# A two-layer graph network: another order of products in the first pair, and TensorE in place of GpSimd and DMA in the last pair

## The chip, the cores and the metric

The kernel runs on one core of one Trainium2 chip. A core has TensorE (PE, matrix products), VectorE (DVE), ScalarE (ACT) and GpSimd (POOL), and SyncE (SP), whose queue issues the DMAs here. The metric is the device time of one execution in microseconds. [...]

## What is computed

64 graphs of 256 nodes with 512 features pass through two layers, each with a residual and a normalization over features. All is in 32-bit floats.

```python
def layer0(x, adj):                        # 8 heads of 64
    q, k, v = x @ Wq + bq, x @ Wk + bk, x @ Wv + bv
    scores = einsum('bqhd,bkhd->bhqk', q, k) / sqrt(64)
    attn = softmax(scores + (1 - adj) * -1e9)
    return einsum('bhqk,bkhd->bqhd', attn, v) @ Wo + bo

def layer1(x, adj):
    h = x @ W
    e = leaky_relu((h @ a1)[:, :, None] + (h @ a2)[:, None, :], 0.2)
    att = softmax(e * adj)
    return elu(att @ h + beta * h)

x = layernorm(x + layer0(x, adj))
x = layernorm(x + layer1(x, adj))
```

## The kernel before

**Tiling and stages.** The 64 graphs ("batches") are taken as 32 pairs. A pair is loaded and projected to queries, keys and values together (stages `x`, `q`, `k`, `v`), and then each of its two batches goes through `scores`, `sums` (the denominators of the softmax), `mix` (attention times values), `o` (projection with Wo, added to the residual X and normalized), `logits`, `attention`, `spread` (attention times X) and `u` (times W), after which `finish` applies the elu, adds, normalizes and stores. The digit behind a stage's name is the batch within the pair. The last pair holds batches 62 and 63.

**Seven products for eight.** `project` (its matmuls are at L433) computes a product of two matrices cut in quarters with seven block products, from sums and differences of the quarters. `left` and `right` are lists of seven operands. Products 1, 2 and 3 need untouched quarters on the right; 5 needs the first sum in place, 6 the second, 4 the last, and 7 the very first difference. GpSimd makes the sums of tokens in `token_sums` (L404) in the order t3, t1 (in place), t2, t4. The sums of Wq and Wk are made by VectorE in `streamed` (L366) in the first pair, and kept in memory for the later pairs. Products gather in PSUM accumulators: `ps_chain` takes 1, 6 and 7, `ps_cross` takes 5 and 3, and, where the first pair's queries and keys are made, `ps_second` takes 2 and `ps_fourth` takes 4. Parameter `raw` is true there.

**The plan.** Nothing is issued as it is written. Every operation is entered with `plan.op(engine, ns, function, reads, writes, mode, claims)`, and `Plan.place` settles the order in which all of them are emitted, by a model with durations and lags. For TensorE, each operation has a turn, (pair + `LATER[stage]`, index in `ROUND`), and all but the last `OPEN` = 60 TensorE operations are placed strictly by turn. The last 60 are placed by what can start soonest and, among those, by the longest remaining chain. The other engines' operations are placed when they are ready in the model, by due times that come from TensorE's turns. Buffers come from counted slots by tag (`half` 18, `full` 4, `ps` 8), and an operation can be placed only if all slots that it claims are free. An operation on TensorE with 0 ns and no instruction (as at stages `logits` and `attention`) only claims slots at its turn.

**Sums over keys.** After the scores, VectorE adds the mask (L750), ScalarE takes the exponential (L752), giving `pT` for each head with two blocks of 128 keys, and GpSimd adds the two blocks of each head into `both` (L754). TensorE multiplies `both` with ones to get the denominators (L766), VectorE takes the reciprocal (L778).

**The last batch.** Where `last` holds (batch 63), several steps go by TensorE instead of by memory: the reciprocals are spread over features with a selecting matrix (`ps_inv`, L802); `plain` projects without sums (L492 to L497); the row of logits comes by a transpose (`tr_s`, L933); the attention is transposed by TensorE (`tr_a`, L976) and copied by ScalarE (L979); `ps_y` (L1001) is its spread. For all other batches, batch 62 among them, a row of logits is made by a 32 x 32 transpose on VectorE (L940), a DMA to memory (`line`) and one back to all partitions (`row`); and the attention goes to memory (`square`, L983), comes back in four DMAs (`att_b`, L986), and is transposed in blocks by VectorE (L990). Where `last` holds, the two halves of the nodes also go through the logits' softmax apart.

**Constants of the second layer.** `second_layer_constants` clears `diag_sb` on GpSimd (L530), writes beta on its diagonal on VectorE (L532), and derives `wa_sb` from W and a.

**At the end** a check of the range of the softmax's sums decides whether a general form runs over all pairs again; with these inputs it doesn't.

Of the kernel before, what the change touches and what calls it, by code (L numbers as in the profile page):

```python
# [12 lines left out]
ALU = mybir.AluOpType  # L13
# [3 lines left out]
P = 128  # L17
# [9 lines left out]
         "o0": 0, "o1": 1, "logits0": 0, "logits1": 1, "attention0": 1, "attention1": 1, "spread0": 1, "spread1": 2,  # L27
         "u0": 1, "u1": 2}
SAFE = 1e15

# [23 lines left out]
class Plan:  # L54
# [12 lines left out]
    LATER = 15000.0  # L67
    OPEN = 60

# [158 lines left out]
def gnn_two_layers(ctx: ExitStack, tc: tile.TileContext, x, adj, Wq, bq, Wk, bk, Wv, bv, Wo, bo, W, a, beta, out):  # L228
    nc = tc.nc
# [128 lines left out]
    def streamed(w, w_dram, name):  # L358
# [3 lines left out]
        s1, s2, s3, s4 = ((lambda n=n: S[n][A]) for n in (1, 2, 3, 4))  # L362
        for n, to, p, m, op, reads in ((3, s3, w11, w21, ALU.subtract, [w]), (1, s1, w21, w22, ALU.add, [w]),
                                       (2, s2, s1, w11, ALU.subtract, [w, S[1]]),
                                       (4, s4, w12, s2, ALU.subtract, [w, S[2]])):
            plan.op("DVE", 700, lambda to=to, p=p, m=m, op=op: nc.vector.tensor_tensor(to(), p(), m(), op), reads,  # L366
                    [S[n]])
# [45 lines left out]

    def project(left, right, by_feature, claims, copy, add, inner=2, width=P, raw=False):

# [33 lines left out]
        copy((0, 0), pe(1, chain, True))  # L449
        if raw:  # L450
            add((0, 0), pe(2, second, True))
            copy((1, 0), pe(4, fourth, True))
        copy((1, 1), pe(5, cross, True))
        if not raw:
            add((0, 0), pe(2, second, True))
        copy((0, 1), pe(6, chain, False))
        add((0, 1), pe(3, cross, False))
        if not raw:
            copy((1, 0), pe(4, fourth, True) if second[1] is None else pe(4, fourth, False, [second]))
        acc = pe(7, chain, False)  # L460
# [68 lines left out]
    def second_layer_constants():  # L529
        plan.op("POOL", 500, lambda: nc.gpsimd.memset(diag_sb[A], 0.0), [], [diag_sb])  # L530
        for t in range(NT):
# [25 lines left out]
    def norm(X, ts):  # L557
# [22 lines left out]
        for i, t in enumerate(ts):  # L580
            plan.op("ACT", 810, lambda i=i, t=t: nc.scalar.activation(  # L581
                X[:, t, :], X[:, t, :], AF.Identity, bias=nm[:, i:i + 1], scale=rs[:, i:i + 1]),
                [nm, rs], [(X, (t, 0)), (X, (t, 1))])

    def pair(m, at, general=False):

        def turn(what):

            plan.turn = ((m or 0) + LATER[what], ROUND.index(what))

# [46 lines left out]
        def qk(left, bias, dst):  # L637
            project(left, right, True, [dst], *gather(
                lambda q: (lambda: dst[:, 2 * q[0]:2 * q[0] + 2, q[1] * N:(q[1] + 1) * N], (dst, q)), bias, True),
                width=N, raw=m == 0)  # L640

# [26 lines left out]
    def batch(m, s, qT, kT, V, dram, general):  # L668

        b = None if m is None else 2 * m + s  # L670
        last = b == B - 1 and not general
        X = sb("x", [NT, D], f"x_{b}")

        def turn(what):
            plan.turn = ((m or 0) + LATER[f"{what}{s}"], ROUND.index(f"{what}{s}"))

# [50 lines left out]
        def attention_by_keys():  # L727
# [6 lines left out]
            def scores(c):  # L734
# [4 lines left out]
                def pe():  # L739
                    for k in range(NT):  # L740
# [5 lines left out]
                plan.op("PE", 870, pe, [(m, (c // 2, j)) for m in (qT, kT) for j in range(NT)], acc, mode="rows",  # L746
                        claims=pT[2 * c:2 * c + 2] + [both[c]])
                for i in range(2):
                    h = 2 * c + i
                    plan.op("DVE", 690, lambda h=h, i=i: nc.vector.tensor_add(pT[h][A], acc[i][A], maskT_sb[A]),  # L750
                            [acc[i], maskT_sb], [pT[h]])
                    plan.op("ACT", 620, lambda h=h: nc.scalar.activation(  # L752
                        pT[h][A], pT[h][A], AF.Exp, scale=1.0 / HD ** 0.5), [pT[h]], [pT[h]])
                    plan.op("POOL", 725, lambda h=h, i=i: nc.gpsimd.tensor_tensor(  # L754
                        both[c][:, i, :], pT[h][:, 0, :], pT[h][:, 1, :], ALU.add),
                        [pT[h]], [(both[c], i)])

            def denominators():
# [4 lines left out]
                def pe():  # L763
                    for i in range(2):
                        for c in range(C):
                            nc.tensor.matmul(acc[32 * c:32 * c + 32, :], ones[:, 16 - 16 * i:48 - 16 * i],  # L766
                                             both[c][:, i, :], start=i == 0, stop=i == 1)

                plan.op("PE", 1000, pe, both, [acc], mode="sums", claims=[inv])

# [156 lines left out]
        turn("logits")  # L927
        if last:
            row = ps([N], "tr_s")
# [18 lines left out]

        for ts in ((0, 1), (1, 2)) if last else ((0, 2),):
            ts, k = slice(*ts), ts[1] - ts[0]  # L950
# [19 lines left out]
        turn("attention")  # L970
        if last:
            tra = ps([NT, N], "tr_a")
# [87 lines left out]

    plan.turn = (B // 2 + 1, 0)
    fine, row, least = st(1, "fine"), ps([P], "row"), st(1, "least")
# [18 lines left out]
    with tc.If(again != 0):  # L1081
# [3 lines left out]
        with tc.For_i(0, B, 2) as i:  # L1085
            for tile_ in stay:
                tile_.parts = {}
            plan = Plan({**slots, "half": slots["half"] - 1})
            pair(None, bass.ds(i, 2), general=True)
            order = plan.place()  # L1090
            with tc.manual_schedule():
                plan.emit(order)
# [29 lines left out]
```

## Time and profile before

| | us |
|---|---|
| median of 3 runs | 2735.23 (2733.61 to 2735.62) |
| time of the profiled execution | 2734.59 |
| its span | 2732.8 |
| TensorE busy | 2698.5 |
| VectorE busy | 1960.9 |
| GpSimd busy | 1728.6 |
| ScalarE busy | 1549.5 |
| mean granted TensorE clock | 0.995 of full |

Times in the profile count from the start of the span. The execution's own time is 1.8 us longer than its span. A line of the timeline reads: start, length, engine, source line, operation, output<-inputs, shapes, count, and in brackets how long the engine was idle before it and what released it. Lengths of grouped matmuls overlap the next group a little, since the end of each is modelled; the distance from start to start is what a group holds the engine. A matmul in 32-bit floats counts as two records.

### The profile page before, as it was taken

What the parts mean: (1) busy time and instruction counts of PE and PEld (TensorE: products, weight loads), DVE (VectorE), ACT (ScalarE), POOL (GpSimd) and SP (SyncE); (2) the same over time, 40 slices, a digit from 0 to 9 for tenths busy, and PEclk for the clock granted to TensorE, in tenths of its full rate; (3) what the DMA queues carried; (4) which work ended last, traced back from release to release, by engine and by line L of the source; (5) the groups of instructions that cost most, each with busy time, mean ns of one, the idle gap of its engine ahead of it and who ended that gap; (6) DMA issues with size and microseconds to landing.
All of it is one profiled execution on the core that took longest, in us unless ns stands there. A gap on an engine that the chain in (4) does not pass through costs nothing. (4 is left out here: it accounts for less than half of the span.)

```text
span 2732.8 us, 47289 instructions
## 1 busy us (share of the span) xinstructions
PE 2698.5 (99%) x15897; PEld 2268.1 (83%) x15897; DVE 1960.9 (72%) x3676; ACT 1549.5 (57%) x3712; POOL 1728.6 (63%) x2261
## 2 busy tenths in 40 slices
PE   9999999999999999999999999999999999999996
PEld 7888888888888888888888888888888888888874
DVE  6777777777777777777777776777777777767674
ACT  3456556556556565565565565655655655656554
POOL 4756666665676666666656766666666566665663
PEclk9999999999999999999999999999999999999998
DMA  8434434344443444343443434443444434343211
GB/s 234 104 101 128 119 97 114 97 121 124 100 120 96 109 128 118 94 113 99 124 124 98 120 90 115 128 113 99 111 101 120 128 96 118 89 120 113 80 55 54
DMA packets 581596, 301.44 MB, mean 110 GB/s; under 512 B 407020, under 2 KB 512356, under 8 KB 581348
## 3 DMA queue, kind: packets, MB, share of 16 engines
q1 hardware_dynamic: 581220, 298.34, 41.7%
q8 instruction: 130, 2.13, 0.3%
q14 instruction: 118, 0.97, 0.1%
q0 software_dynamic: 128, 0.01, 0.0%
HBM read 245.50 MB, written 52.75 MB: 109 GB/s over the span
## 5 line engine op out<-in xcount | busy, mean ns | idle before, releaser
L754 POOL TENSOR_TENSOR both<-pT 128x256 f32<-128x256 f32 x512 | 361.3, 734 | 398.6 <-ACT pT L752 398.6
L750 DVE TENSOR_TENSOR pT<-ps_sc,maskT_sb 128x512 f32<-128x512 f32 x512 | 324.2, 680 | 84.7 <-PE ps_sc L743 84.7
L752 ACT ACTIVATE pT<-pT 128x512 f32<-128x512 f32 x512 | 304.0, 626 | 49.3 <-DVE pT L750 47.4
L917 DVE SCALAR_TENSOR_TENSOR junk<-x,wa_sb 128x512 f32<-128x512 f32 x256 | 207.8, 837 | 110.3 <-ACT x L581 109.2
L743 PE MATMUL ps_sc<-qT,kT 64*128 64x256 f32 x2048 | 238.4, 382 | 0.0
L720 PE MATMUL ps_pv<-pT,v 128*64 128x256 f32 x2048 | 235.1, 382 | 0.0
L743 PEld LDWEIGHTS ps_sc<-qT,kT 64*128 64x128 f32 x2048 | 192.8, 187 | 44.4 <-issue 24.6
L469 ACT COPY u<-ps_chain 128x256 f32<-128x256 f32 x126 | 47.0, 373 | 319.2 <-PE ps_chain L433 318.7
L581 ACT ACTIVATE x<-x,nmr,rs 128x512 f32<-128x512 f32 x256 | 197.6, 808 | 50.2 <-POOL nmr L577 50.0
L720 PEld LDWEIGHTS ps_pv<-pT,v 128*64 128x64 f32 x2048 | 141.3, 137 | 91.0 <-DVE kT L478 12.8
L1026 POOL TENSOR_TENSOR X_sums<-x 128x256 f32<-128x256 f32 x126 | 150.9, 1207 | 99.5 <-ACT x L581 99.5
L564 ACT ACTIVATE junk<-x,mean 128x512 f32<-128x512 f32 x256 | 182.2, 714 | 6.4 <-DVE mean L570 6.4
L564 ACT ACTIVATE junk<-x 128x512 f32<-128x512 f32 x256 | 159.4, 625 | 36.5 <-DVE x L894 33.7
L704 POOL TENSOR_TENSOR x<-x,res_sb 128x512 f32<-128x512 f32 x128 | 176.3, 1380 | 0.0
L575 POOL TENSOR_SCALAR rs<-sq 128x2 f32<-128x2 f32 x130 | 34.9, 269 | 194.3 <-ACT junk L564 189.0
L404 POOL TENSOR_TENSOR oS<-oT 128x256 f32<-128x256 f32 x126 | 92.1, 731 | 84.2 <-DVE mean L570 52.5
L816 DVE TENSOR_TENSOR oT<-oT,inv_all 128x512 f32<-128x512 f32 x126 | 134.7, 1107 | 0.0
L955 POOL TENSOR_TENSOR e<-e,adj_sb 128x512 f32<-128x512 f32 (+1 forms) x65 | 81.6, 1255 | 80.7 <-DVE e L952 76.8
L433 PE MATMUL ps_chain<-sw_sb,yS 128*128 128x256 f32 x504 | 129.3, 379 | 0.0
L433 PE MATMUL ps_chain<-so_sb,oS 128*128 128x256 f32 x504 | 129.3, 379 | 0.0
L778 DVE RECIPROCAL inv<-ps_den 128x256 f32<-128x256 f32 x64 | 112.5, 1757 | 17.1 <-PE ps_den L766 8.7
L404 POOL TENSOR_TENSOR yS<-yT 128x256 f32<-128x256 f32 x126 | 92.6, 735 | 48.5 <-DVE yT L478 32.2
(240 smaller groups left out, 7164.5 us busy)
## 6 DMA issues: line engine op xcount, KB each, us to landing
x<-in_x_dram SPq DMA_DIRECT2D x64, 512.0 KB
out_dram<-x SPq DMA_DIRECT2D x128, 256.0 KB
inv_all<-rows SPq DMA_DIRECT2D x126, 256.0 KB
xin<-in_x_dram SPq DMA_DIRECT2D x248, 128.0 KB
wq_sums<-wq_sums SPq DMA_DIRECT2D x124, 256.0 KB
wk_sums<-wk_sums SPq DMA_DIRECT2D x124, 256.0 KB
wq_sums<-in_L_gnn_Wq_dram SPq DMA_DIRECT2D x93, 256.0 KB
wk_sums<-in_L_gnn_Wk_dram SPq DMA_DIRECT2D x93, 256.0 KB
```

What stands on the lines that cost most here:

```text
L404: plan.op("POOL", 180 + 545 * width // P, lambda: nc.gpsimd.tensor_tensor(dst(), p(), m(), ALU.subtract), reads, writes)
L433: nc.tensor.matmul(dst[:, f, :], lhs, rhs, start=start and f == 0 and c == 0, stop=c == inner - 1, skip_group_check=True)
L564: plan.op("ACT", 700, lambda: nc.scalar.activation(junk[A], X[:, t, :], func, bias=mean[:, i:i + 1] if bias else 0.0, accum_out=to[:, i:i ...
L581: plan.op("ACT", 810, lambda i=i, t=t: nc.scalar.activation(X[:, t, :], X[:, t, :], AF.Identity, bias=nm[:, i:i + 1], scale=rs[:, i:i + 1] ...
L704: plan.op("POOL", 1270, lambda t=t: nc.gpsimd.tensor_tensor(X[:, t, :], X[:, t, :], res_sb[A], ALU.add), [res_sb], tokens(t))
L720: nc.tensor.matmul(acc[r * HD:(r + 1) * HD, i, :], V[:, 2 * k + s, h * HD:(h + 1) * HD], pT[h][:, k, :], start=k == 0, stop=k == NT - 1)
L743: nc.tensor.matmul(acc[j][:, k, :], kT[r:r + HD, c, key_blk(k)], own(qT, r, c), start=True, stop=True)
L750: plan.op("DVE", 690, lambda h=h, i=i: nc.vector.tensor_add(pT[h][A], acc[i][A], maskT_sb[A]), [acc[i], maskT_sb], [pT[h]])
L752: plan.op("ACT", 620, lambda h=h: nc.scalar.activation(pT[h][A], pT[h][A], AF.Exp, scale=1.0 / HD ** 0.5), [pT[h]], [pT[h]])
L754: plan.op("POOL", 725, lambda h=h, i=i: nc.gpsimd.tensor_tensor(both[c][:, i, :], pT[h][:, 0, :], pT[h][:, 1, :], ALU.add), [pT[h]], [(bot ...
L917: plan.op("DVE", 780, lambda t=t, i=i, junk=junk: nc.vector.scalar_tensor_tensor(junk[A], X[:, t, :], 1.0, wa_sb[:, i, :], op0=ALU.mult, o ...
L1026: plan.op("POOL", ns, lambda: nc.gpsimd.tensor_tensor(dst(), p(), m(), op), reads, writes)
```

## The change

There are four parts.

1. In the first pair, queries and keys take their products in the order 1, 2, 5, 6, 4, 3, 7; before it was 1, 2, 4, 5, 6, 3, 7. `raw` is now called `first`. VectorE makes the sums of Wq and Wk in the order s1, s2, s4, s3 (before: s3, s1, s2, s4). The clearing of `diag_sb` reads `w_sb`, so it waits for that weight's load.
2. For batch 63, TensorE sums over all keys itself: the denominators take both blocks of every `pT` (16 matmul calls for 8), and GpSimd's additions into `both` are not made.
3. What `last` meant for the logits and the attention now holds where `near` does, for both batches of the last pair: row of logits and transposed attention by TensorE, softmax by halves. The spread, projections and finish of batch 62 stay as they were.
4. A tuple `FINISH` writes out the order of the last stages as (stage, pairs before the last); these stages get turns from it by `take_turn`. `OPEN` is 70 instead of 60.

```diff
+FINISH = (("sums1", 1), ("mix1", 1), ("scores0", 0), ("v", 0), ("attention0", 1), ("spread1", 2), ("sums0", 0), ("u1",
+          2), ("mix0", 0), ("scores1", 0), ("o1", 1), ("logits1", 1), ("o0", 0), ("attention1", 1), ("u0", 1),
+          ("spread1", 1), ("logits0", 0), ("spread0", 1), ("sums1", 0), ("mix1", 0), ("attention0", 0), ("spread0",
+          0), ("o1", 0), ("attention1", 0), ("u1", 1), ("u0", 0), ("logits1", 0), ("spread1", 0), ("u1", 0))
...
-    OPEN = 60
+    OPEN = 70
...
-        for n, to, p, m, op, reads in ((3, s3, w11, w21, ALU.subtract, [w]), (1, s1, w21, w22, ALU.add, [w]),
-                                       (2, s2, s1, w11, ALU.subtract, [w, S[1]]),
-                                       (4, s4, w12, s2, ALU.subtract, [w, S[2]])):
+        for n, to, p, m, op, reads in ((1, s1, w21, w22, ALU.add, [w]), (2, s2, s1, w11, ALU.subtract, [w, S[1]]),
+                                       (4, s4, w12, s2, ALU.subtract, [w, S[2]]), (3, s3, w11, w21, ALU.subtract, [w])):
...
         copy((0, 0), pe(1, chain, True))
-        if raw:
+        if first:
             add((0, 0), pe(2, second, True))
-            copy((1, 0), pe(4, fourth, True))
         copy((1, 1), pe(5, cross, True))
-        if not raw:
+        if not first:
             add((0, 0), pe(2, second, True))
         copy((0, 1), pe(6, chain, False))
-        add((0, 1), pe(3, cross, False))
-        if not raw:
-            copy((1, 0), pe(4, fourth, True) if second[1] is None else pe(4, fourth, False, [second]))
+        if not first:
+            add((0, 1), pe(3, cross, False))
+        copy((1, 0), pe(4, fourth, True) if second[1] is None else pe(4, fourth, False, [second]))
+        if first:
+            add((0, 1), pe(3, cross, False))
         acc = pe(7, chain, False)
...
-        plan.op("POOL", 500, lambda: nc.gpsimd.memset(diag_sb[A], 0.0), [], [diag_sb])
+        plan.op("POOL", 500, lambda: nc.gpsimd.memset(diag_sb[A], 0.0), [w_sb], [diag_sb])
...
+    def take_turn(m, what):
+        at_end = (what, B // 2 - 1 - m) if m is not None else None
+        if at_end in FINISH:
+            plan.turn = (B // 2 + 1, FINISH.index(at_end))
+        else:
+            plan.turn = ((m or 0) + LATER[what], ROUND.index(what))
...
+        near = m == B // 2 - 1 and not general
...
-                        claims=pT[2 * c:2 * c + 2] + [both[c]])
+                        claims=pT[2 * c:2 * c + 2] + ([] if last else [both[c]]))
...
-                    plan.op("POOL", 725, lambda h=h, i=i: nc.gpsimd.tensor_tensor(
-                        both[c][:, i, :], pT[h][:, 0, :], pT[h][:, 1, :], ALU.add),
-                        [pT[h]], [(both[c], i)])
+                    if not last:
+                        plan.op("POOL", 725, lambda h=h, i=i: nc.gpsimd.tensor_tensor(
+                            both[c][:, i, :], pT[h][:, 0, :], pT[h][:, 1, :], ALU.add),
+                            [pT[h]], [(both[c], i)])
...
-                    for i in range(2):
-                        for c in range(C):
-                            nc.tensor.matmul(acc[32 * c:32 * c + 32, :], ones[:, 16 - 16 * i:48 - 16 * i],
-                                             both[c][:, i, :], start=i == 0, stop=i == 1)
-
-                plan.op("PE", 1000, pe, both, [acc], mode="sums", claims=[inv])
+                    for k in range(NT if last else 1):
+                        for i in range(2):
+                            for c in range(C):
+                                nc.tensor.matmul(
+                                    acc[32 * c:32 * c + 32, :], ones[:, 16 - 16 * i:48 - 16 * i],
+                                    pT[2 * c + i][:, k, :] if last else both[c][:, i, :],
+                                    start=i == 0 and k == 0, stop=i == 1 and (k == NT - 1 or not last))
+
+                if last:
+                    plan.op("PE", 1500, pe, pT, [acc], mode="sums", claims=[inv])
+                else:
+                    plan.op("PE", 1000, pe, both, [acc], mode="sums", claims=[inv])
...
         turn("logits")
-        if last:
+        if near:
             row = ps([N], "tr_s")
...
-        for ts in ((0, 1), (1, 2)) if last else ((0, 2),):
+        for ts in ((0, 1), (1, 2)) if near else ((0, 2),):
...
         turn("attention")
-        if last:
+        if near:
             tra = ps([NT, N], "tr_a")
```

More of the change, by code (lines that the diff above doesn't have):

```diff
@@ L412, in token_sums, with project @@
                 (q[0, 1], keys(0, 1)), (t2, [(S, 0)]), (t3, [(S, 1)])]
-    def project(left, right, by_feature, claims, copy, add, inner=2, width=P, raw=False):
+    def project(left, right, by_feature, claims, copy, add, inner=2, width=P, first=False):
         shape = [2, width] if by_feature else [width // P, F]
@@ L583, in norm @@
                 [nm, rs], [(X, (t, 0)), (X, (t, 1))])
+    def take_turn(m, what):
[4 more added lines that the diff above has]
+            plan.turn = ((m or 0) + LATER[what], ROUND.index(what))
     def pair(m, at, general=False):
         def turn(what):
-            plan.turn = ((m or 0) + LATER[what], ROUND.index(what))
+            take_turn(m, what)
         def dram(ap, s):
@@ L639, in qk @@
                 lambda q: (lambda: dst[:, 2 * q[0]:2 * q[0] + 2, q[1] * N:(q[1] + 1) * N], (dst, q)), bias, True),
-                width=N, raw=m == 0)
+                width=N, first=m == 0)
         if m == 0:
@@ L671, in batch @@
         last = b == B - 1 and not general
+        near = m == B // 2 - 1 and not general
         X = sb("x", [NT, D], f"x_{b}")
         def turn(what):
-            plan.turn = ((m or 0) + LATER[f"{what}{s}"], ROUND.index(f"{what}{s}"))
+            take_turn(m, f"{what}{s}")
         def tokens(t):
@@ L1058, in gnn_two_layers @@
         pair(m, slice(2 * m, 2 * m + 2))
-    plan.turn = (B // 2 + 1, 0)
+    plan.turn = (B // 2 + 2, 0)
     fine, row, least = st(1, "fine"), ps([P], "row"), st(1, "least")
@@ L1088, in gnn_two_layers @@
             plan = Plan({**slots, "half": slots["half"] - 1})
+            plan.OPEN = 60
             pair(None, bass.ds(i, 2), general=True)
```

## The prediction

> **What bounds the kernel.** First I read the page's table of engines and its chain, then TensorE's instructions in order of time at both ends, then its waits.
>
> ```profile
> span 2732.8 us, 47289 instructions
> ...
> PE 2698.5 (99%) x15897; PEld 2268.1 (83%) x15897; DVE 1960.9 (72%) x3676; ACT 1549.5 (57%) x3712; POOL 1728.6 (63%) x2261
> ...
> PE 1%; DVE 0%; ACT 0%; POOL 0%; issue 0%; POOLq 0%; DVEq 0%; ACTq 0%
> ```
>
> TensorE (PE) is idle for 34 us in 2733, and the chain that ended last covers only the last 2% of the span. From 100 to 300 and from 2500 to 2640 us the windows show it fully busy, and the page's slices between show no gap. So an order of work can pay only at the two ends, where the change lies. First the opening, as TensorE's timeline and the windows of 2 us (window, length, busy time and count of PE, PEld, DVE, ACT, POOL, then granted clock, DMA share, GB/s):
>
> ```profile
> 10.04 2.24 PE L433 MATMUL ps_second<-xT,wq_sb 128*128 128x256 f32 x8
> 14.33 3.66 PE L433 MATMUL ps_fourth<-xS,wq_sb 128*128 128x256 f32 x8 [2.04 <-POOL xS L404]
> 17.83 1.89 PE L433 MATMUL ps_cross<-xT,wq_sums_s 128*128 128x256 f32 x8
> ```
> ```profile
> 12.00:14.00 2.00, 0.29 (x2) 0.00 (x0) 1.97 (x2) 0.00 (x0) 1.92 (x2) 1.00 1.06 409
> 14.00:16.00 2.00, 1.67 (x4) 1.40 (x5) 1.97 (x3) 0.00 (x0) 0.97 (x2) 0.58 1.04 402
> 16.00:18.00 2.00, 2.00 (x6) 1.61 (x6) 2.00 (x3) 0.00 (x0) 1.92 (x2) 0.56 1.07 392
> ```
>
> Product 4 waits 2.04 us for GpSimd's fourth token sum and then runs at clock 0.58 to 0.56: it holds PE 3.50 us (14.33 to 17.83), where eight records at full clock take 1.73 (17.83 to 19.56). Then the end, from the same timeline:
>
> ```profile
> 2629.28 3.72 PE L743 MATMUL ps_sc<-qT,kT 64*128 64x256 f32 x32
> ...
> 2658.26 1.07 PE L766 MATMUL ps_den<-both,ones 128*32 128x256 f32 x16
> 2662.18 2.94 PE L802 MATMUL ps_inv<-inv,select 128*128 128x256 f32 x8 [2.85 <-DVE select L783]
> ...
> 2678.18 0.68 PE L433 MATMUL ps_chain<-attT,x 128*128 128x128 f32 x4 [2.49 <-DVE attT L990]
> ...
> 2695.54 6.21 PE L1001 MATMUL ps_y<-attT,x 128*128 128x256 f32 x16 [0.68 <-ACT attT L979]
> ...
> 2717.07 1.03 PE L433 MATMUL ps_chain<-sw_sb,yS 128*128 128x256 f32 x4
> ```
>
> Call T0 the end of the last scores, 2632.93 us. The last matmul ends at T0+85.2; the last batch but one (62) then finishes in 14.7 us, and the span ends at T0+99.9. Full-clock PE work in those 85.2 us, from the spacing of starts: five projections by features or logits at 6.05 (30.3), three spreads at 3.1 (9.3), mixing 3.6, denominators 1.0, ps_inv 8 x 0.216 = 1.7, four plain halves at 3.45 (13.8), ps_y 16 x 0.216 = 3.5, small transposes 1.4: **64.6 us**. So 20.6 us are idleness or a slow clock (ps_inv takes 2.94 for 1.7, ps_y 6.21 for 3.5).
>
> **Part 1, opening.** Order 1, 2, 5, 6, 4, 3, 7 for 1, 2, 4, 5, 6, 3, 7; VectorE makes s1, s2, s4, s3 for s3, s1, s2, s4; the diagonal's clearing waits for w_sb, which takes the two diagonal writes (DVE L532, 1.20 us, started at 10.29 after beta's DMA) from before them. The last stall for wq_sb ends at 10.72. s1 starts there and takes 1.75 beside GpSimd, as L366 at 11.41 does: 12.5. s2 (1.63): 14.15. s4 (0.69): 14.85; s3 by 16.5. GpSimd's sums end at 9.86, 11.22, 12.61 and 14.28 now. Product 2 ends at 12.1. So 5 runs 12.55 to 14.28, 6 to 16.0, 4 to 17.7, 3 to 19.5, 7 to 21.2, against 24.74 now: **-3.5 us**. wk's subtractions follow directly on VectorE (17.75 to 22.86 now, some 2 us earlier then), ahead of k's fifth product at about 25.1. Behind this the queues hold the same work; PE's small stalls at 62 and 87 us (0.54 and 0.28) stay.
>
> Here a rule is weighed against a row. The Trainium skill, "TensorE: Matmul & The Clock Gate", in "What's actually happening", has the clock halve after about 3.4 us of idleness. By that, the 2.04 us stall would cost only itself and the change give 1.6 (2.04 less the 0.45 that remains before product 5). The row shows 0.58 after 2.04 us, so I add 1.8. The trace decides; 1.5 is kept as the lower end, and no idleness at all (-4.1) as the upper.
>
> The clearing of the diagonal sits on GpSimd's in-order queue behind a DMA issued at 32.7 to 35.8. Behind it would stand the sums over keys of the first scores (7 at 40.09). From the GB/s of the slices, w_sb lands near 40. These sums end at 46.7 and are read at 53.30: 6.6 us of cover, 3.1 after the earlier start. Price nothing; if it lands 5 us later than I think, 2 us.
>
> **Part 2, added and removed at the end.** Batch 63's sums over keys: 16 more records at 1.07/16: +1.0 on PE; gone are eight GpSimd adds (8 x 0.734 = 5.9 us) and four of 18 "half" slots that `inv` competed for. Batch 62's row of logits: +0.35 (tr_s: 0.34 in the chain); its attention: four transposes, +0.8 (tr_a: 2 x 0.41). **PE +2.2 us: 66.8.** ScalarE gets a copy (0.59), VectorE loses two transposes (0.24 and 0.70) and gains the split by halves (three extra short instructions, about 0.8); both lie beside PE.
>
> Off the path go batch 62's two trips through memory. Its scalars: svT ends at 2666.34, z starts at 2677.96: 11.6 us, of which the row's DMA stands behind four att_b issues in SP's queue. Its attention: e ends at 2686.30, attT is made at 2699.70: 13.4. A second rule here: the Trainium skill, "DMA: Bandwidth & Descriptors", in "Anatomy of one DMA", gives about 2.0 us fixed to a DMA (its fit is for another issuing path); two trips of two would be some 8 us. The rows show 25.0, since they hold the queue, the other engine's turn and the second wait. In their place come 0.8 and 1.4 us (tr_s to z; e to attT at 2695.49 of batch 63). So batch 62 is some 22 us earlier and no longer last.
>
> **Part 3, the order.** Up to the last scores it holds the same stages, so T0 moves only with the opening. Sums of 62 now stand before u of 60 (6 us earlier). Between spread of 60 and its u there is then 1.0 us of sums where products read sums that GpSimd makes: two yT adds and two GpSimd sums are about 2.4 us, less 1.0 and the first product's 0.86: a stall of 0.5 on PE. Behind T0 one projection (o of 61) stays fixed and 70 rather than 60 operations are placed by the longest remaining chain. Batch 63's own chain, unhindered, from the rows: exponentials ready at T0+6.5, sums 2.0, mixing and ps_inv 5.4, product 0.9, plain 6.9, norm 5, dots 1.4, softmax 6.0, attT 1.5, ps_y 3.5, copies 0.9, plain 6.9: PE done at T0+47. Now its sums come at T0+25.3. Batch 61's chain keeps its DMA: attention at T0+42 to 45, then about 12.8 to the end of u and 14.7: T0+72. So neither chain but **PE's work** is the bound: 66.8 and what idleness remains. I take 5 us of idleness, since until T0+42 only some 40 us of work can be ready and stages of 63 still meet VectorE and ScalarE, each about 55 us busy behind T0. Then the finish: 14.7 if a projection ends it, 12.2 if 63's plain product does (7.7 from 2712.83 to 2720.51, and 4.5 from the last normalization to the span's end): 13.5. Sum 66.8 + 5 + 13.5 = 85.3 for 99.9: **-14.6**. Bounds: idleness 1 and 12.2 give 80.0 (-19.9); idleness 12 and 14.7 give 93.5 (-6.4).
>
> **Sum.** -3.5 - 14.6 + 0.5 = -17.6. The profiled execution's time is 2734.59, 1.8 above its span, and 0.64 below the median; from the median 2735.23 I get 2717.6, in round numbers **2718 us**.
>
> **Rivals.**
> A. The tail is held by slots: batch 63's mixing takes a "full" slot, and now starts at 2654.66 as u of 60 has ended. If the order doesn't release one sooner, sums stay near T0+25. For: mixing came before the sums, as a queue for slots would have it. Against: spread of 60 moves behind, and four halves are freed. Batch 63's end then stays near T0+93 (2720.51+4.5), less 3.3 for the spread that stood before its last product (4.2, copies hide 0.9): about 90 with some cold clock as now, -10, but 62's spread and u (9.2) take perhaps half of it back: -5, with the opening -8: 2727.
> B. It doesn't do what it says: the chain through 61's DMA takes the gain at the end, or 62 and 63 now meet on VectorE and ScalarE (both 70% busy in a tail of 80 us). Then opening alone: 2732.
> C. Slower: SP's queue is in order, and 61's row, square and four att_b stand in it among outputs that wait for their batch. If 61's attT comes late, all later is late: attT at 2678.03 now leads to 27.5 us more. It decides from attT at T0+75.7 (99.9 + 3.3 - 27.5), 31 us later than now; by 40 us, +9: 2744. For: issues of 61 stood 1.1 to 4 us in that queue. Against: nothing in the trace waits for SP by tens of us.
>
> **Chances.** Forecast 0.73, A 0.14, B 0.08, C 0.05. Range 2709 to 2729: from -24 (both best ends) with 2 us for what I can't see, to A with its own 2 us. A measurement of this kernel can't tell changes within 0.2% (5.5 us). Faster: forecast, and nearly all of A: 0.86; same: B and the rest: 0.09; slower: 0.05.
>
> **What would show it.** Opening: product 5 directly behind 2, no clock below 1.0 from 12 to 18, the first ps_sc near 34 rather than 37.36. Sums of 63 within 12 us of T0; no line or square DMA for 62; ps_inv and ps_y near 1.7 and 3.5 us; last matmul near T0+72. Wrong if PE is idle for 12 us or more behind T0, or if another wait of several us stands between 100 us and T0.

## The result and the profile after

| | before | after |
|---|---|---|
| median of 6 runs (lowest to highest), us | 2734.31 (2732.43 to 2735.62) | 2720.05 (2719.03 to 2722.51) |
| span of the profiled execution, us | 2732.8 | 2718.3 |
| first score product (ps_sc) starts | 37.36 | 33.99 |
| T0, the end of the last scores | 2632.93 | 2631.01 |
| denominators of batch 63 start | T0+25.3 | T0+14.3 |
| last matmul ends | T0+85.2 | T0+75.2 |
| from there to the end of the span | 14.7 | 12.1 |

The ratio of the medians is 0.995 with a 95% interval of 0.9937 to 0.9963: the changed kernel is faster by 14.3 us, and the spans differ by 14.5. T0 moved by 1.9 us, the part behind T0 shrank from 99.9 to 87.3, by 12.6.

The page of the changed kernel, its table of engines and its chain:

```profile
span 2718.3 us, 47307 instructions
...
PE 2696.2 (99%) x15919; PEld 2268.6 (83%) x15919; DVE 1956.4 (72%) x3677; ACT 1548.9 (57%) x3713; POOL 1721.8 (63%) x2254
...
PE 97%; DVE 1%; POOL 0%; ACT 0%; issue 0%; DMA 0%; SPq 0%; ACTq 0%; POOLq 0%; DVEq 0%
```

TensorE does slightly less busy time in a shorter span: 22 us are left in which it is idle, against 34. TensorE's timeline at the opening (start, length, engine, line, output from inputs, tile, count; an idle time ahead of a row would stand in brackets):

```profile
11.01 1.89 PE L437 MATMUL ps_second<-xT,wq_sb 128*128 128x256 f32 x8
12.74 1.89 PE L437 MATMUL ps_cross<-xT,wq_sums_s 128*128 128x256 f32 x8
14.46 1.89 PE L437 MATMUL ps_chain<-xS,wq_sums_s 128*128 128x256 f32 x8
16.19 1.89 PE L437 MATMUL ps_fourth<-xS,wq_sb 128*128 128x256 f32 x8
```

Products 2, 5, 6 and 4 start 1.72 to 1.73 us apart, with no bracket. The windows of 2 us from 8 to 20 show a granted clock of 1.00 in every one (for the time up to 10.36 see below, at e4). The same timeline behind T0:

```profile
2631.01 1.13 PE L437 MATMUL ps_chain<-wo_sb,oT 128*128 128x256 f32 x4
...
2645.36 1.93 PE L781 MATMUL ps_den<-pT,ones 128*32 128x256 f32 x32
2647.22 3.67 PE L733 MATMUL ps_pv<-pT,v 128*64 128x256 f32 x32
2650.82 1.99 PE L822 MATMUL ps_inv<-inv,select 128*128 128x256 f32 x8
...
2669.92 0.41 PE L996 MATMUL tr_a<-ident,e 128*128 128x128 f32 x2 [1.41 <-DVE rc L983]
2670.51 0.41 PE L996 MATMUL tr_a<-ident,e 128*128 128x128 f32 x2 [0.18 <-DVE e L986]
2672.39 0.91 PE L437 MATMUL ps_chain<-attT,x 128*128 128x128 f32 x4 [1.47 <-ACT attT L999]
...
2694.72 3.69 PE L1021 MATMUL ps_y<-attT,x 128*128 128x256 f32 x16
...
2704.28 1.88 PE L502 MATMUL ps_plain<-w_sb,yT 128*128 128x512 f32 x4
```

Batch 63's denominators come 11 us sooner, ps_inv and ps_y run without a wait and at full pace (before: 2.94 and 6.21 us), and the last product is 63's own plain one. One hole is left, from 2668.4 to 2672.4, and two waits of half a microsecond. The waits of 2.85, 1.94, 2.49, 1.53, 1.24 and 0.68 us, which stood behind T0 before, are gone. SyncE's queue of DMA issues shows what is left of the trips through memory:

```profile
2646.54 0.59 SPq L961 DMA_DIRECT2D line<-svT  x1
2648.33 0.33 SPq L963 DMA_DIRECT2D row<-line  x1
2665.89 0.37 SPq L1003 DMA_DIRECT2D square<-e  x1
2668.25 2.61 SPq L1006 DMA_DIRECT2D att_b<-square  x4
```

They are batch 61's alone; batch 62 has none.

### The profile page after: what moved, and what is told of

The parts are those of the page before. It is cut to its first block, busy times and chain, and to the rows that moved or that the text cites. A ratio compares the mean times of both kernels' runs of the same rounds, so it can differ in the third digit from the quotient of the medians.

```text
span 2718.3 us, 47307 instructions
## 1 busy us (share of the span) xinstructions
PE 2696.2 (99%) x15919; PEld 2268.6 (83%) x15919; DVE 1956.4 (72%) x3677; ACT 1548.9 (57%) x3713; POOL 1721.8 (63%) x2254
## 3 DMA queue, kind: packets, MB, share of 16 engines
q8 instruction: 130, 2.13, 0.3%
## 4 chain that ended last, share of the span: by engine, by line
PE 97%; DVE 1%; POOL 0%; ACT 0%; issue 0%; DMA 0%; SPq 0%; ACTq 0%; POOLq 0%; DVEq 0%
PE ps_chain L437 33%; PE ps_cross L437 22%; PE ps_pair L437 10%; PE ps_sc L756 8%; PE ps_pv L733 8%; PE ps_second L437 6%; PE ps_fourth L437 6%; PE ps_den L781 2%; DVE junk L543 0%; DMA xin<-in_x_dram 0%; ACT junk L569 0%; DMA row<-line 0%; SPq L631 0%; PE ps_y L1021 0%; PE ps_plain L502 0%
## 5 line engine op out<-in xcount | busy, mean ns | idle before, releaser
L768 POOL TENSOR_TENSOR both<-pT 128x256 f32<-128x256 f32 x504 | 354.6, 731 | 383.1 <-ACT pT L765 383.1
L580 POOL TENSOR_SCALAR rs<-sq 128x2 f32<-128x2 f32 (+1 forms) x130 | 34.8, 268 | 208.8 <-ACT junk L569 203.5
L975 POOL TENSOR_TENSOR e<-e,adj_sb 128x512 f32<-128x512 f32 (+1 forms) x66 | 82.2, 1247 | 77.0 <-DVE e L972 77.0
L798 DVE RECIPROCAL inv<-ps_den 128x256 f32<-128x256 f32 x64 | 112.5, 1758 | 18.5 <-ACT junk L794 9.3
```

## The experiments

All times are medians with their ratio to the kernel before, measured on the same chip beside it (its own median there was 2733.89 to 2734.43). "Full" is the changed kernel, 2720.05. The profiled execution of each kernel gives the middle columns.

| kernel | parts | median, us | ratio (95%) | 63's denominators | PE idle behind T0 | last matmul | finish |
|---|---|---|---|---|---|---|---|
| before | none | 2734.31 | 1 | T0+25.3 | 12.4 | T0+85.2 | 14.7 |
| e1_opening | 1 | 2731.49 | 0.9992 (0.9983 to 1.0001) | 25.3 | 12.4 | 85.2 | 14.8 |
| e3_sums | 2 | 2731.30 | 0.9990 (0.9983 to 0.9997) | 25.6 | 12.1 | 83.7 | 14.1 |
| e2_near | 3 | 2728.68 | 0.9980 (0.9972 to 0.9987) | 25.6 | 9.1 | 81.4 | 13.8 |
| e4_order | 4 | 2731.64 | 0.9989 (0.9980 to 0.9998) | 25.4 | 11.1 | 82.2 | 14.6 |
| e8_no_near | 1, 2, 4 | 2738.82 | 1.0017 (1.0010 to 1.0024) | 25.3 | 14.7 | 87.0 | 18.5 |
| e6_no_order | 1, 2, 3 | 2725.68 | 0.9969 (0.9957 to 0.9980) | 21.9 | 9.1 | 79.6 | 11.7 |
| e11_open70 | 1, 2, 3, OPEN | 2724.39 | 0.9961 (0.9946 to 0.9975) | 21.5 | 8.2 | 78.9 | 12.3 |
| e7_no_sums | 1, 3, 4 | 2724.28 | 0.9961 (0.9947 to 0.9975) | 25.4 | 8.1 | 79.6 | 12.2 |
| e15_sums_slots | e7, slots | 2720.55 | 0.9951 (0.9934 to 0.9967) | 16.9 | 5.9 | 75.7 | 12.2 |
| after | 1 to 4 | 2720.05 | 0.9950 (0.9937 to 0.9963) | 14.3 | 4.2 | 75.2 | 12.1 |
| e13_products | full, sums back | 2719.52 | 0.9947 (0.9931 to 0.9964) | 14.3 | 4.8 | 73.1 | 12.0 |
| e12_near61 | full, 61 too | 2720.34 | 0.9949 (0.9933 to 0.9966) | 14.3 | 4.5 | 73.7 | 13.8 |
| e16_search | e12, slots, order | 2715.00 | 0.9930 (0.9913 to 0.9946) | 10.4 | 1.7 | 64.0 | 11.6 |

### One part alone: e1, e2, e3, e4

Each puts one part of the change into the kernel before. e1:

```diff
-            copy((1, 0), pe(4, fourth, True))
...
+        copy((1, 0), pe(4, fourth, True) if second[1] is None else pe(4, fourth, False, [second]))
+        if first:
+            add((0, 1), pe(3, cross, False))
```

> Part 1 alone on the kernel before: another order of the first pair's products, VectorE's order of the weight sums, the later clearing of the diagonal. My theory (stall of product 4 and the slow clock behind it): first scores near 34.0 us of the span for 37.36, some of it lost again in small stalls on the way, last scores of the last pair end 2.5 to 3.4 us before 2632.93, and the span ends as much earlier: 2729.5 to 2730.5. Rival (the end is set by other things than TensorE's queue, such as the DMAs of the last stages): the opening gains 3.4, the end less than 1: about 2732.5.

e2:

```diff
+        near = m == B // 2 - 1 and not general
...
-        if last:
+        if near:
```

> Part 3 alone: batch 62's row of logits and its attention by TensorE, order and sums as before. My theory (batch 62's two trips through memory are what ends last): batch 62 is finished some 20 us earlier, batch 63's plain products end the kernel, span 2722 to 2727. Rival (slots and the model's order hold the tail, not the DMAs): gain below 3, about 2731.

e3:

```diff
+                if last:
+                    plan.op("PE", 1500, pe, pT, [acc], mode="sums", claims=[inv])
```

> Part 2 alone: batch 63's sums over keys by TensorE, no additions on GpSimd, the four slots of these sums free. My theory: batch 63's denominators come sooner, but batch 62 with its DMAs still ends last, so within 1.5 us of before, plus or minus: 2731.5 to 2734.5. Rival (the slots were what held the tail): denominators within 15 us of the last scores and 5 us or more gained: 2728 or less.

e4:

```diff
-    OPEN = 60
+    OPEN = 70
...
+            take_turn(m, what)
```

> Part 4 alone: the written order of the last stages and 70 rather than 60 operations placed freely; batch 62 still by DMA, sums by GpSimd. My theory: denominators of 62 come about 6 us earlier and with them all of batch 62, whose two trips through memory still end last: gain 4 to 7 us, span 2726 to 2729. Rival (the order brings most of the whole change's tail by itself): 11 us or more, 2722 or less. Second rival: the order was made for the other parts and without them costs: slower than 2733.

Measured: -2.6, -5.4, -2.8 and -2.4 us, a sum of 13.1 for 14.3. That the sum is near doesn't make the parts independent: in none of the four do 63's denominators come before T0+25.3, and in the full change they come at T0+14.3. What made them come is in no part alone.

Against what was expected: e2's span of 2726.9 lies just inside the range. e4 gained 2.4 us and not 4 to 7. e3 gained a little more than forecast, but its denominators did not come sooner, which was the reason given. e1's median fits its range, though its interval just reaches 1; its trace does not, since the profiled execution was its slowest (2733.66), with the first scores at 36.14 and T0 only 1.0 us sooner.

These kernels also say something on the clock in the opening. e2, e3 and e4 have the old opening, each in an execution of its own. TensorE's timeline of e4:

```profile
8.67 3.31 PE L437 MATMUL ps_chain<-xT,wq_sb 128*128 128x256 f32 x8
11.81 1.89 PE L437 MATMUL ps_second<-xT,wq_sb 128*128 128x256 f32 x8
15.61 1.99 PE L437 MATMUL ps_fourth<-xS,wq_sb 128*128 128x256 f32 x8 [1.91 <-POOL xS L408]
```

The wait for the fourth token sum is there, 1.91 us for 2.04, but product 4 then holds PE 1.83 us (15.61 to 17.44), not 3.50, at clock 1.00. In e2 and e3 the waits are 1.75 and 1.29, with the same clock behind them. What differs is when the clock is decided. In each trace its records change only on a grid of 3.413 us, which lies elsewhere in each execution. Here are two steps of that grid before, and two in e4 (window, length, busy time and count of PE, PEld, DVE, ACT, POOL, granted clock, DMA share, GB/s):

```profile
10.92:14.33 3.41, 1.37 (x6) 0.86 (x5) 3.38 (x4) 0.00 (x0) 3.20 (x3) 1.00 1.06 407
14.33:17.74 3.41, 3.41 (x8) 2.78 (x9) 3.38 (x4) 0.00 (x0) 2.35 (x2) 0.50 1.05 401
```
```profile
11.36:14.77 3.41, 2.34 (x11) 1.71 (x9) 3.34 (x3) 0.84 (x2) 3.25 (x3) 1.00 1.05 405
14.77:18.18 3.41, 2.57 (x12) 2.29 (x13) 3.41 (x3) 0.54 (x2) 3.14 (x3) 1.00 1.06 399
```

Before, the stall lies whole in one step: PE is idle for 2.04 of 3.41 us, and the next step runs at half the clock. In e4 a boundary cuts the stall into 1.07 and 0.84 us, and the clock stays. In all fourteen traces, steps at full clock with up to 1.83 us of idleness were followed by full clock and those with 1.99 us or more by half; of two between, 1.88 us was followed by half (e6) and 1.89 by full (e4).

In those three, product 1 is stretched instead (3.14 us in e4, 2.13 before). The changed kernel has such a product 1 too, as its row and the durations of its records show (in ns, shortest/median/longest); the third row is product 4 of the kernel before, at half the clock:

```profile
8.05 3.12 PE L437 MATMUL ps_chain<-xT,wq_sb 128*128 128x256 f32 x8
```
```profile
L437 PE MATMUL ps_chain<-xT,wq_sb x8: 379/619/797, 8.1 to 10.8; 128*128 128x256 f32 x8
```
```profile
L433 PE MATMUL ps_fourth<-xS,wq_sb x8: 514/634/794, 14.3 to 17.5; 128*128 128x256 f32 x8
```

The column of the granted clock reads 1.00 over product 1, but the trace has no record of the clock ahead of 10.36 us in the changed kernel, 11.36 in e4 and 7.50 before. By their durations the stretched records ran at half the clock until then. In e2 and e3, waits of 0.25 and 0.69 us for wq_sb come on top.

From the start of product 1 to the first scores it is 29.45 us before, 28.30 to 28.47 in e2, e3 and e4, 25.94 after, and 25.65 to 27.31 in the nine other kernels with the new order. The first scores start at 36.73 to 37.36 us with the old order (mean of four 37.0) and at 33.92 to 36.14 with the new one (mean of ten 34.8). So the new order is worth about 2.2 us by the traces and 2.6 by e1's medians, and 3.5 only against the one execution that I worked from.

### One part undone: e8, e6, e7

> Parts 1, 2 and 4; batch 62 still by memory. My theory (its two trips of 11.6 and 13.4 us are on the path that ends last): most of the tail's gain is lost, span 2725 to 2729. Rival (batch 62 is early enough in the new order to hide them): 2720 or less.

> Parts 1, 2 and 3 without the written order (ROUND and 60 free operations as before). My theory (the tail is one schedule; batch 62's DMAs had to go before the other parts can pay, and the order only lets batch 63 start sooner): opening -2 to -3, near -5.4 as measured alone, sums little: span 2722 to 2726, so 4 to 8 us behind the full change. Rival (the parts simply add, each as alone): 2734.05 - 2.6 - 5.4 - 2.7 = 2723.3, minus 1.6 = span 2721.7. Second rival (order unneeded): within 2 us of the full change's 2718.3.

> Parts 1, 3 and 4; batch 63's key sums stay with GpSimd and its four slots. My theory (with the new order batch 63's denominators come some 14 us behind the last scores, and GpSimd's additions can be done by then): within 3 us of the full change, span 2717 to 2721. Rival (the four half slots keep the denominators back as before, to 20 us and more behind the last scores): 5 us or more lost, 2723 and above.

The edits are the full change with `if last:` back for `if near:` (e8), without `FINISH` and with `OPEN = 60` (e6), and with `both` summed by GpSimd and read by TensorE for batch 63 too (e7).

**Without part 3 the other three make the kernel slower than before** (e8, +4.4 us), where I had expected most of the gain to be lost (a span of 2725 to 2729 us; it is 2736.4). TensorE's timeline, its windows, one row of VectorE's timeline and SyncE's queue in e8:

```profile
2683.42 1.20 PE L436 MATMUL ps_chain<-attT,x 128*128 128x128 f32 x4 [7.12 <-issue]
```
```profile
2672.00:2676.00 4.00, 4.00 (x14) 2.31 (x13) 2.96 (x7) 2.33 (x7) 0.19 (x1) 1.00 0.49 86
2676.00:2682.60 6.60, 0.31 (x1) 0.00 (x0) 5.60 (x13) 5.39 (x16) 3.72 (x8) 0.71 0.01 2
2683.00:2687.00 4.00, 2.99 (x10) 2.62 (x11) 2.48 (x7) 1.77 (x3) 2.89 (x6) 0.50 0.40 146
```
```profile
2682.62 0.70 DVE L1008 STREAM_TRANSPOSE attT<-att_b 128x512 f32<-128x512 f32 x1
```
```profile
2669.91 0.37 SPq L1001 DMA_DIRECT2D square<-e  x1
...
2672.04 2.63 SPq L1004 DMA_DIRECT2D att_b<-square  x4
...
2685.08 0.38 SPq L1001 DMA_DIRECT2D square<-e  x1
2687.38 2.59 SPq L1004 DMA_DIRECT2D att_b<-square  x4
```

TensorE stands for 7.1 us until attT of 61 is made, and goes on at half the clock. "issue" names no releaser, but the product reads attT. Memory isn't all of that wait: the DMA engines, busy for 0.49 of the time from 2672 to 2676, are idle from there on (0.01), and attT is made only at 2682.62, behind work for 62 and 63 on VectorE (busy for 5.60 of 6.60 us). Batch 62's trip follows from 2685.08, fifteen us behind 61's, and its attention is made at 2698.0: it ends last, with a finish of 18.5. The written order has put 61 and 62 where nothing else is left to run beside them. This is akin to my third rival, with a smaller delay (61's attention is used at T0+52.5, the rival decided from T0+75.7) but for both batches, one behind the other.

Without part 4 (e6) 5.6 us of the gain are lost, as expected (4 to 8). Without part 2 (e7) it is 4.2, where I had expected less than 3 and the rival with the slots 5 or more. In both the denominators are late again. TensorE's timeline of e7:

```profile
2657.18 1.07 PE L778 MATMUL ps_den<-both,ones 128*32 128x256 f32 x16
2661.54 3.55 PE L814 MATMUL ps_inv<-inv,select 128*128 128x256 f32 x8 [3.29 <-DVE select L795]
...
2669.20 1.19 PE L496 MATMUL ps_plain<-wo_sb,oT 128*128 128x256 f32 x2 [3.41 <-DVE oT L825]
```

ps_den starts at T0+25.4, where it was before, though the order names the same stages; u of 60 has been used up ahead of it, so nothing fills TensorE while VectorE makes the reciprocals (3.29 us) and the features (3.41), and ps_inv then takes 3.55 us.

### Which of part 2's two gifts counts: e15, and which of part 4's: e11

Part 2 takes 5.9 us of additions from GpSimd and frees four "half" slots. e15 is e7, GpSimd's additions and all, with `both` of the last batch in another set of slots:

```diff
-            both = [sb("half", [2, N], "both") for c in range(C)]
+            both = [sb("piece" if last else "half", [2, N], "both") for c in range(C)]
```

> Parts 1, 3 and 4, with GpSimd's sums over keys of batch 63 kept, but put in four slots of another tag that is idle at the end, so the four half slots are free as in the full change. If the slots hold the denominators back: they come 14 to 16 us behind the last scores, span 2718 to 2720. If GpSimd's additions themselves, or the planner's rule that a change of TensorE's mode waits until nothing else is ready, hold them: 20 us and more behind the last scores, span 2721.5 to 2724. After the runs before I expect the second.

Its timeline:

```profile
2647.24 1.07 PE L778 MATMUL ps_den<-both,ones 128*32 128x256 f32 x16
2651.84 1.99 PE L814 MATMUL ps_inv<-inv,select 128*128 128x256 f32 x8
```

The 16 calls of the old form, fed by GpSimd, start at T0+16.9 instead of T0+25.4, ps_inv needs no wait, and 3.7 of the 4.2 us are back. I had expected the other outcome. So it is the slots that held batch 63, not the additions. The sums by TensorE are worth what is left, 0.5 us, which these runs can't tell from nothing.

e11 has the parts 1 to 3, the old order and `OPEN = 70`:

> Parts 1, 2 and 3 and 70 free operations, but turns by ROUND as before, so spread of batch 60 and o of 62 keep their place and the sums of 62 stand behind u of 60. Theory (what counts is that batch 63's stages may go ahead of the two batches before): within 2 us of the full change, span 2717 to 2720.5. Rival (the written order with the sums of 62 six us earlier counts): 3 to 6 us behind it, 2721 to 2724.

It is 4.3 us behind the full change, as the rival had it and not my theory, and 1.3 below e6 (five runs against seven, with ranges that overlap). The looser bound does little when it is added first (the denominators come at T0+21.5); the written order on top of it does the rest.

### VectorE's order in the opening: e13

```diff
-        for n, to, p, m, op, reads in ((1, s1, w21, w22, ALU.add, [w]), (2, s2, s1, w11, ALU.subtract, [w, S[1]]),
-                                       (4, s4, w12, s2, ALU.subtract, [w, S[2]]), (3, s3, w11, w21, ALU.subtract, [w])):
+        for n, to, p, m, op, reads in ((3, s3, w11, w21, ALU.subtract, [w]), (1, s1, w21, w22, ALU.add, [w]),
+                                       (2, s2, s1, w11, ALU.subtract, [w, S[1]]),
+                                       (4, s4, w12, s2, ALU.subtract, [w, S[2]])):
...
-        plan.op("POOL", 500, lambda: nc.gpsimd.memset(diag_sb[A], 0.0), [w_sb], [diag_sb])
+        plan.op("POOL", 500, lambda: nc.gpsimd.memset(diag_sb[A], 0.0), [], [diag_sb])
```

> The full change, but VectorE makes the weights' sums in the order of before (s3, s1, s2, s4) and the diagonal is written ahead of them as before; only the order of the products is new. My theory: s1 is ready at about 14.9 us as before, product 5 waits for it from 12.1 to 12.7 on, some 2.2 to 2.8 us idle, and the clock then halves as behind the stall before (0.58 there): first scores at 37.0 to 37.5, span 3 us above the full change. Rival [...]: only the wait is lost, no granted clock below 1.0 behind it, first scores near 36.2.

My expectation fell. VectorE's timeline of e13, and TensorE's row of product 5:

```profile
10.31 0.88 DVE L538 TENSOR_SCALAR diag_sb<-ident,beta_sb 128x128 f32<-128x128 f32 x2 [10.31 <-DMA beta_sb<-in_L_gnn_beta_dram]
11.33 1.54 DVE L371 TENSOR_TENSOR wq_sums_s<-wq_sb 128x512 f32<-128x512 f32 x1
12.90 1.64 DVE L371 TENSOR_TENSOR wq_sums_s<-wq_sums_s,wq_sb 128x512 f32<-128x512 f32 x1
```
```profile
13.54 1.89 PE L438 MATMUL ps_cross<-xT,wq_sums_s 128*128 128x256 f32 x8
```

s1 (it reads wq_sb alone) is still made first and s2, which reads s1 as well, behind it: the plan places these operations by when they are due, and the order in which the code names them decides nothing. The kernel before shows the same in its own trace, since the second of these rows reads a sum that the first has made:

```profile
11.41 1.75 DVE L366 TENSOR_TENSOR wq_sums_s<-wq_sb 128x512 f32<-128x512 f32 x1
13.19 1.63 DVE L366 TENSOR_TENSOR wq_sums_s<-wq_sums_s,wq_sb 128x512 f32<-128x512 f32 x1
```

So its sums ran as s1, s2, s4, s3 already, with s1 ready at 13.16 us and not at the 14.9 that I had expected, and the change did not reorder them. In e13, the two diagonal writes are back before them, s1 is done at 12.87 instead of 12.10, and product 5 still starts directly behind product 2. The median is that of the full change (2719.52). Product 2 ended later in this execution (product 5 starts at 13.54 for 12.74), so that s1 had the time. Of part 1, the order of the products is the only piece whose effect can be told from nothing here.

### The last hole, and a faster version: e12, e16

Is the hole at 2668 to 2672 in the changed kernel made by 61's trip through memory? e12 gives 61 what 62 got:

```diff
-        near = m == B // 2 - 1 and not general
+        near = not general and b >= B - 3
```

> The full change, with row of logits and attention by TensorE for batch 61 too. If TensorE's hole from 2668.35 to 2672.39 us and the slow clock up to 2680 come from batch 61's attention being still on its way through memory (made at 2675.53 to 2676.23): the hole closes, some 3 us of idleness and 4 of slow clock go, 1.2 us of transposes come, span 2712 to 2715. Rival (the planner then uses up its ready work sooner, as it did without the written order, and the hole moves): 2718 to 2722.

It gains nothing that can be measured (2720.34), as the rival had it. The last matmul ends 1.4 us sooner behind T0 and the finish is 1.6 longer, since a projection ends the work in place of the plain product; TensorE is idle for 4.5 us, in eight small waits in place of one hole.

e16 also moves z, e and attT of these batches to other slots, and writes another order, with `OPEN = 83` and due times shifted stage by stage:

```diff
+        tag = "piece" if near else "half"
+        z, e = sb(tag, [NT, N], "z"), sb(tag, [NT, N], "e")
+        attT = sb(tag, [NT, N], "attT")
...
-            due[n] = last - rest[n] if n in tail else min(due[n], last - rest[n])
+            due[n] = last - rest[n] + shift.get(n, 0.0) if n in tail else min(due[n], last - rest[n])
```

> As the run before, and the slots for the softmax and attention of batches 61 to 63 in the idle tag, another written order of the last stages, 83 free operations and shifts of due times by stage, found by trying orders against the planner's own count of the end. If TensorE's idleness behind the last scores is all that is left: idleness below 2 us, span 2712 to 2716. Rival (such an order is made for the planner's durations and the chip's differ by as much): 2717 to 2720.

2715.00 us: 5 us below the full change, as expected, and the fastest kernel here. TensorE's timeline:

```profile
2648.13 1.93 PE L836 MATMUL ps_den<-pT,ones 128*32 128x256 f32 x32
...
2655.17 1.99 PE L877 MATMUL ps_inv<-inv,select 128*128 128x256 f32 x8 [0.91 <-DVE select L858]
```

The last scores end at 2637.68, since a projection of features (seven products with wo_sb and so_sb from 2624.09) now runs ahead of them; batch 63 then goes through with 0.91 us as its longest wait, and PE is idle for 1.7 us in all behind T0. What is left is PE's own work and the finish of 11.6 us. Which of its four edits brings how much was not taken apart.

## Why the prediction was right

I forecast 2718 us and the median is 2720.05, inside the range. By the terms of the sum, against the profiled executions (spans 2732.8 and 2718.3):

| term | predicted | measured |
|---|---|---|
| opening, to the first scores | -3.5 | -3.4 |
| stall in u of 59 (the prediction says of 60) | +0.5 | +0.5 |
| between the first scores and there | 0 | +0.9 |
| last matmul behind T0 (85.2): PE's work 66.8, and idle or slow | 66.8 + 5 = 71.8: -13.4 | 66.8 + 8.4 = 75.2: -10.0 |
| finish (14.7) | 13.5: -1.2 | 12.1: -2.6 |
| sum (the measured one from the spans) | -17.6 | -14.5 |

**Opening.** Products 5, 6, 4, 3 and 7 ran as written down, with the first scores at 33.99 for "near 34". That the figure fits so well is luck: ten executions with the new order have the first scores from 33.92 to 36.14. I took the slow clock behind the 2.04 us stall as a part of the stall's price, 1.8 us; the same stall in e2, e3 and e4 is followed by full clock. The Trainium skill's "TensorE: Matmul & The Clock Gate" (section "What's actually happening"), which I set aside for the row, has the clock judged in free-running windows of about 3.4 us. The traces agree on the window (steps of 3.413 us in all fourteen), and so a stall of this length can fall whole into one or be cut in two. They differ on what halves it: the page names an idle window, and here 2.04 us of idleness within one were enough. By the rule I would have taken 1.6, by the row 3.5; 2.2 to 2.6 is what the runs show. And the reordering of VectorE's sums, which I priced within this term, is none: they ran in that order before.

**The middle.** I held that the queues behind the first scores hold the same work. At equal instructions the lead is 3.4 us at the first scores, 3.1 at 62 us, where a wait on VectorE's pT is 0.88 instead of 0.54 us, 2.5 from about 900 us on, where a row's DMA stands in the chain, and 1.9 behind the stall in u of 59. That is the 1.1 us by which T0 moved less than forecast. In e12, e13 and e16 the lead stays constant within 0.05 us from 100 us on up to that stall: the loss at 900 us is no property of the change, as far as these show.

**Slots, my rival A.** The mechanism is real: 63's denominators start at T0+25.3 to 25.6 in seven kernels with quite different orders, and in e7 it is the four slots that keep them there. I gave it 0.14 because four halves go free, and that is the point on which it was decided (e7 against e15, 8.5 us for the denominators and 3.7 for the median). What I hadn't seen is that the halves of part 2 are not enough alone: e3 and e8 have them and stay at 25.6 and 25.3. Part 3 has to be there too, and then the order: with both of these and the old order (e6) the denominators come at T0+21.9, with the written one at T0+14.3. I take it that 62's shorter logits and attention give their own halves back sooner; that was not tried by itself.

**The tail.** PE's work is the bound, as forecast, and its waits (4.2 us) kept within the 5 us that I allowed. The term that was mis-sized is the slow clock, which the forecast of the tail put at nothing. Steps of the clock's grid around the hole, in the changed kernel and then in e13, whose instructions of TensorE behind T0 are the same in the same order:

```profile
2669.35:2672.76 3.41, 1.19 (x7) 0.78 (x8) 3.14 (x9) 2.92 (x6) 1.85 (x4) 1.00 0.49 77
2672.76:2676.17 3.41, 2.82 (x11) 2.27 (x10) 3.38 (x7) 1.81 (x6) 3.01 (x6) 0.50 0.00 0
2676.17:2679.59 3.42, 3.42 (x17) 3.33 (x15) 0.06 (x1) 1.93 (x7) 2.94 (x8) 0.50 0.00 0
```
```profile
2666.84:2670.26 3.42, 2.02 (x10) 1.47 (x9) 2.49 (x9) 2.60 (x8) 3.17 (x7) 1.00 0.31 62
2670.26:2673.67 3.41, 1.98 (x12) 1.34 (x12) 3.26 (x7) 2.92 (x7) 1.57 (x3) 1.00 0.25 39
2673.67:2677.09 3.42, 2.25 (x16) 2.15 (x16) 2.66 (x6) 2.06 (x6) 3.02 (x7) 1.00 0.00 0
```

In the changed kernel PE is busy for 1.19 of 3.41 us in one step, and two steps at half the clock follow, with 6.2 us of its work in them, which costs about 3.1. With the 4.2 us of listed waits that is 7.3 of the 8.4. In e13 the waits add up to more (4.8 us), but no step has over 1.44 us of idleness, the clock stays full, and the last matmul ends at T0+73.1 instead of T0+75.2. So how the waits fall into the steps, which no plan here has in hand, moved this end by about 2 us.

What makes the hole itself is read from the trace and not tried by a run. In the first two of these steps VectorE is busy for 6.5 of 6.8 us: the softmax of 62 (e done at 2670.36), the finish of 60 and dot products of 63 share it. The copy of 62's attT then stands behind a normalization of 63 on ScalarE (2671.05 to 2671.86; the copy starts at 2671.77). This is the meeting on VectorE and ScalarE that I had in rival B and in the 5 us. 61's attention comes back in the same moments (made from 2675.53, T0+44.5; forecast T0+42 to 45) but is not what PE waits for; e12 agrees, since without this trip nothing is gained. In the finish I took the middle of two ends, 14.7 and 12.2; 63's plain product ended last, and it is the lower one. That error (1.4 us too long) and the tail's (3.4 too short) offset each other in part: the size of the sum, -17.6 for -14.5, owes something to luck.

**Small ones.** The clearing of the diagonal ran at 43.26 for 0.52 us behind the sums over keys and nothing waited for it. ps_inv and ps_y hold PE 1.84 and 3.53 us (forecast 1.7 and 3.5). Two figures of the forecast don't come out of its own rows: with no idleness at all the opening would give -4.0, not -4.1, and 2720.51 + 4.5 is T0+92.1, not T0+93. Neither moves the forecast.

## What to carry to other kernels

An end whose work is all on one engine is won by having another batch's work ready for every wait in it, so look first for what holds that work back: here it was four buffer slots, which no list of waits shows and which were found as a start time that didn't move whatever else was changed. Parts of such a change are to be tried by leaving each out as well as by putting each in alone: every part alone gained 2 to 5 us, and the three without `near` lost 4.4. A slow clock that one execution shows behind a stall of two us is to be looked for in a second execution before it enters a sum.

## What the runs showed of the hardware

- In all fourteen traces the granted clock is full or half and changes only on a grid of 3.413 us (in the changed kernel at 10.36 and at 2672.76, 780 steps later). A step at full clock with 1.99 us or more of idleness of TensorE was followed by half clock, one with up to 1.83 us by full clock. The first record of full clock comes at 7.50 to 13.35 us.
- So a stall at one place costs more in some executions than in others: 2.04 us was followed by half the clock over 3.5 us of work, 1.91, 1.75 and 1.29 us at the same place by full clock in three others. In the tail, waits of 1.41, 0.18, 1.47 and 0.59 us came with two steps at half clock in the changed kernel, and waits of 1.40, 0.18, 0.87 and 1.54 us at the same places with none in e13.
- A round trip of two dependent small DMAs through memory, from the end of the instruction that made the data to the start of the one that used it, took 9.7 us both times for batch 61 in the changed kernel (svT to z, 2646.50 to 2656.23, and e to attT, 2665.84 to 2675.53), 11.6 and 13.4 us for batch 62 in the kernel before. The DMA engines were idle again 5.3 and 6.4 us after the start for 61, and 6.1 us into the 13.4 for 62; behind that came VectorE's other work. TensorE's transposes in their place (tr_s and tr_a of batch 62) hold it for 0.38 and 0.82 us.
- Product 1 of the opening took 2.13 us before and 2.37 to 4.13 us in the thirteen other executions, where its records are as long as at half clock up to the first record of the clock.
